# A sparse graph layer with gathered tiles: lists of 128-row tiles for any set of column groups, and products in one form

## The chip, the cores and the metric

One core of one Trainium2 chip. The metric is the device time of one execution in microseconds (us): the median of the runs of a kernel, taken beside runs of the other kernel on the same chip.

## The reference, cut to what matters

```
A_norm = relu((A + A.T) * 0.5)                 # A: 4096 x 4096, sparse, diagonal present
D = sum(A_norm, axis=1);  d = D ** -0.5        # 0 where D is 0
L_norm = I - d[:, None] * A_norm * d[None, :]
HW = einsum('bnf,fo->bno', x, W)               # x: 8 x 4096 x 256, W: 256 x 256
out = relu(einsum('nm,bmo->bno', L_norm, HW))
x = layernorm(x + out)                         # over the last 256 columns
```

The chance of an entry in A falls with the row's and the column's number, so the first rows are dense and most later ones thin. All numbers are f32.

## The kernel before

N = 4096 nodes are 32 blocks of 128. The 8 x 256 columns of HW are one row of G = 2048 numbers (8 KB) for each node, called g once it is scaled by d. An output block is the product of a 128-column strip of A (transposed, one row for each node m) with g; only nodes with an entry in the strip count.

**First part.** A is loaded in pieces of 512 x 512, symmetrised (transposes on PE, sums on DVE, L512 to L521) and written back to DRAM as `a_dram` (L523 and on). Beside it DVE and POOL keep `uses`: one flag for each row and each group of 32 columns. HW is formed (L596 to L645) and written as `g_dram`. Output block 0, the densest, is summed on the way as `lead` (L583). The lists of the first units are made here too, in pieces that are called by number (`due`, `run_due`, L676).

**Second part.** The other 31 blocks are handled in 16 units of two blocks, in the order SEQ. A unit has up to eight groups of 32 columns, four in each of its blocks b0 and b1. For each unit a list says which rows m are fetched and in which slot, so that rows that serve the same groups stand together. A tile is 128 slots. POOL fetches a tile by two indirect DMAs: `ga` (L1032: of each listed row of `a_dram`, 32, 128 or 256 columns, by `owner`) and `g` (L1047: the rows of g, 1 MB). Tiles lie in a ring of RING = 12 slots. The first blocks of g, which every unit needs, are kept on chip (`g_hub`, HUBS = 2 blocks in each unit); their strips of A, `gh`, come by small DMAs that POOL issues when the unit before has used the old ones (L1020).

A unit is a row of *steps*. A step is a list of products (t, half, b, j, w): tile t, rows of one half or of all 128, block b, w groups from group j. Each step runs them for four chunks of 512 columns (L1257 to L1270), so that a step fills the array of PE once for each chunk: one product of 128x128, two of 128x64, four of 128x32, two of 64x128, four of 64x64 or eight of 64x32. On the chip each f32 product shows as two instructions. `steps_of` (L878 to L937 and on) picks the forms: it looks at the next REACH = 8 tiles and takes the shape that fills the array best. Hub steps are woven between the others.

Before a unit starts, its lists are made on DVE and PE, several units ahead: `patterns` (which groups a row serves, as a number; then which of 15 KINDS of sets it belongs to), `count` (two products that rank the rows of each kind, L298), `place` (each row gets a slot in one of its kinds' half-tiles of L = 64 rows; rows that overflow go on to a pair or to a whole block by `offer`, L328), `count_rest` and `place_rest` (what is left over goes to tiles that serve all groups), `spread`, `collect` and `index` (slots are turned into row numbers by products with one-hot matrices, L450). The tables CAPS and FIRST give the half-tiles of each kind in each unit. Numbers that these need are written by small fills on POOL in the first part (`set_constants`, L215). At a unit's end, behind the last step with b0, PE gets the list products (`lists`, L1211).

After each step `gather_ahead` (L1057) asks for one more tile, or for two where more than SLACK = 5 slots are free; each request waits for that step's products. The results of a block are copied out of PSUM by ACT (`evict`, L788), and DVE does the residual and the layer norm.

If a list does not fit (`over`), a dense path computes everything again; for this input it does not run.

Of the kernel before, what the change touches and what calls it, by code (L numbers as in the profile page):

```python
# [9 lines left out]
F32 = mybir.dt.float32  # L10
# [11 lines left out]
KINDS = [15, 1, 4, 2, 8, 16, 64, 32, 128, 240, 51, 204, 60, 195, 0]  # L22
# [3 lines left out]
HUBS = [2] * 16  # L26

CAPS = [
# [16 lines left out]
]  # L45

FIRST = [
# [16 lines left out]
]  # L64
# [3 lines left out]
def kernel(  # L68
# [41 lines left out]
    RING = 12  # L110
    REACH = 8
    TAIL = 4
    SLACK = 5
    LONG = 28
    EPS = 1e-5
    NK = len(KINDS)
    L = 64
    mid = KINDS.index(16), KINDS.index(51)
    NL = NK - 1

# [4 lines left out]
    def upto_tile(u, ks):  # L125
        return max((FIRST[u][k] + CAPS[u][k] + 1) // 2 for k in ks)

    tiles = [upto_tile(u, range(NK)) for u in range(NU)]

    def owners(u, t):  # L130

        kinds_at = [k for k in range(NK) for s in (2 * t, 2 * t + 1) if FIRST[u][k] <= s < FIRST[u][k] + CAPS[u][k]]
        masks = [KINDS[k] or 255 for k in kinds_at]
        if all(m & (m - 1) == 0 for m in masks):
            return ALONE
        low, high = any(m & 15 for m in masks), blocks(u) == 2 and any(m >> QU for m in masks)
        return 2 if low and high else int(high)

    ALONE = 3
    owner = [[owners(u, t) for t in range(tiles[u])] for u in range(NU)]  # L140
    alone = [[t for t in range(tiles[u]) if owner[u][t] == ALONE] for u in range(NU)]
    tmax = max(tiles)
# [1257 lines left out]
```

## Time and profile before

| | |
|---|---|
| runs | 1496.15, 1495.63, 1490.57 us; median 1495.63 |
| profiled execution | 1496.15 us, span of the profile 1496.2 |
| first gathered product | 587 us |
| last product | 1484 us |
| PE busy, span | 1420.1 us (95%) |
| DMA | 540.52 MB, 361 GB/s on the mean |

The times in the prediction come from the one profiled execution. PE rows are matrix products, PEld rows the loads of their weights, which lie beside them. In rows of products by form, 128*32 is the part of the array that an instruction uses: rows by columns. Busy time is what the profile models for a product; products of different columns of the array lie beside each other, so a mean of 600 ns with four beside each other is not 600 ns of PE each.

### The profile page before, as it was taken

To read this page: it belongs to the slowest core of one execution; us is meant where nothing else is said; L and a number is where in the kernel's file an instruction comes from. 1 tells how busy PE (TensorE), PEld (TensorE's weight loads), DVE (VectorE), ACT (ScalarE), POOL (GpSimd) and SP (SyncE) were. 2 spreads that over 40 slices of the span, in tenths; PEclk is the share of its full clock that TensorE was granted. 3 is DMA by queue.
4 is the path that set the end of the run, shared out by engine and by line. 5 is a ranking of instruction groups with operands and counts; after the bars stand their busy time and mean duration, and the time that the engine had idled before them with its cause. 6 is when DMAs were issued, how large, how long until landed. Compare 5 with 4: busy or idle time off the path is not lost.

```text
span 1496.2 us, 20479 instructions
## 1 busy us (share of the span) xinstructions
PE 1420.1 (95%) x6768; PEld 757.9 (51%) x6768; DVE 1025.2 (69%) x3010; ACT 368.7 (25%) x462; POOL 745.6 (50%) x1547
## 2 busy tenths in 40 slices
PE   7998988979999999999999999999999999998996
PEld 6777877766777764333333334333333333333342
DVE  4767558889596752356569678789898079797454
ACT  4555545434544460010100100100110011001102
POOL 2444010010322336756577677577677646666762
PEclk9999999989999999999999999999999999999998
DMA  9999999999999999979899899999999979988995
GB/s 340 360 377 381 406 346 337 393 385 338 379 356 341 371 392 373 373 270 379 332 377 379 338 402 407 366 388 403 398 382 377 387 259 341 354 316 321 402 404 220
DMA packets 215265, 540.52 MB, mean 361 GB/s; under 512 B 17751, under 2 KB 107527, under 8 KB 180839
## 3 DMA queue, kind: packets, MB, share of 16 engines
q0 software_dynamic: 53808, 281.94, 48.5%
q1 hardware_dynamic: 93200, 126.62, 24.4%
q10 hardware_dynamic: 68144, 130.58, 23.0%
q8 instruction: 56, 0.92, 0.2%
q14 instruction: 57, 0.46, 0.1%
HBM read 425.72 MB, written 136.34 MB: 376 GB/s over the span
## 4 chain that ended last, share of the span: by engine, by line
PE 62%; DMA 14%; DVE 11%; issue 7%; POOL 3%; ACT 3%; ACTq 0%; another core or an unknown queue 0%; DVEq 0%; POOLq 0%; SPq 0%
PE py L1263 45%; PE pg L627 8%; DMA a_dram<-sym 6%; DVE sym L520 4%; DMA g<-g_dram,gi 3%; PE xtr L616 3%; PE lead L585 3%; PE tr L516 3%; DMA xin<-in_x_dram 2%; POOL ga L1032 2%; ACT sym L524 1%; DVE sums L527 1%; POOL g L1047 1%; DMA g_dram<-held 1%; PE lists L450 1%
## 5 line engine op out<-in xcount | busy, mean ns | idle before, releaser
L1263 PE MATMUL py<-g,ga 128*32 128x512 f32 (+4 forms) x2880 | 644.8, 606 | 12.3 <-DMA g<-g_dram,gi 7.2
L1263 PEld LDWEIGHTS py<-g,ga 128*32 128x32 f32 (+4 forms) x2880 | 226.0, 138 | 402.0 <-issue 374.4
L1032 POOL DMA_INDIRECT ga<-a_dram,ai x256 | 277.6, 1084 | 181.3 <-issue 62.2
L1047 POOL DMA_INDIRECT g<-g_dram,gi x256 | 284.5, 1111 | 92.9 <-issue 77.6
L788 ACT ACTIVATE y<-py,minus_r 128x512 f32<-128x512 f32 x120 | 80.2, 686 | 796.3 <-PE py L1263 545.9
L627 PE MATMUL pg<-w_sb,xt 128*128 128x256 f32 x1024 | 233.4, 387 | 6.5 <-ACT xt L617 5.7
L1263 PE MATMUL py<-g_hub,gh 128*128 128x512 f32 x496 | 226.6, 601 | 0.5 <-DVE low L465 0.3
L627 PEld LDWEIGHTS pg<-w_sb,xt 128*128 128x128 f32 x1024 | 196.9, 195 | 34.5 <-ACT xt L617 6.6
L520 DVE TENSOR_TENSOR sym<-tr,adj 128x512 f32<-128x512 f32 x256 | 162.3, 684 | 59.0 <-PE tr L516 54.1
L527 DVE TENSOR_REDUCE sums<-sym 128x64 f32<-128x2048 f32 x64 | 145.7, 2282 | 69.5 <-ACT sym L524 69.5
L528 POOL TENSOR_SCALAR uses<-sums 128x64 uint8<-128x64 f32 x64 | 26.7, 417 | 271.1 <-DVE sums L527 236.9
L516 PE MATMUL tr<-ident,adj 128*128 128x128 f32 x1024 | 137.1, 281 | 20.5 <-DVE sym L520 14.3
L1263 PEld LDWEIGHTS py<-g_hub,gh 128*128 128x128 f32 x496 | 90.5, 190 | 123.6 <-issue 116.8
L524 ACT ACTIVATE sym<-sym 128x2048 f32<-128x2048 f32 x64 | 122.7, 1917 | 122.8 <-DVE sym L520 118.6
L516 PEld LDWEIGHTS tr<-ident,adj 128*128 128x128 f32 x1024 | 115.8, 143 | 50.9 <-DVE sym L520 31.1
L242 DVE TENSOR_TENSOR_SCAN incl_r<-carry,lists 128x32 f32<-128x32 bf16 x13 | 2.9, 221 | 182.0 <-PE lists L397 176.0
L429 DVE TENSOR_TENSOR hot<-iota_q,at 128x1024 bf16<-128x1024 f32 x64 | 74.5, 1220 | 34.0 <-PE lead L585 32.1
L798 DVE TENSOR_TENSOR xr<-xr,y 128x2048 f32<-128x2048 f32 x31 | 70.8, 2284 | 38.8 <-ACT y L788 32.1
L616 PE MATMUL xtr<-ident,xin 128*128 128x128 f32 x512 | 74.5, 299 | 17.9 <-DVE sym L520 9.0
L831 DVE TENSOR_SCALAR xr<-xr,mv,root 128x256 f32<-128x256 f32 x248 | 85.1, 416 | 1.1
L807 DVE BATCH_NORM_STATS2 stats<-xr 128x6 f32<-128x256 f32 x248 | 84.0, 413 | 1.1
L585 PE MATMUL lead<-gt,strip 128*128 128x512 f32 x176 | 82.4, 593 | 0.0
(164 smaller groups left out, 1040.1 us busy)
## 6 DMA issues: line engine op xcount, KB each, us to landing
adj<-in_adj_dram SPq DMA_DIRECT2D x64, 1024.0 KB
a_dram<-sym ACTq DMA_DIRECT2D x64, 1024.0 KB
out_dram<-xr SPq DMA_DIRECT2D x31, 1024.0 KB
xr<-in_x_dram ACTq DMA_DIRECT2D x28, 1024.0 KB
xin<-in_x_dram SPq DMA_DIRECT2D x44, 512.0 KB
g_dram<-gt ACTq DMA_DIRECT2D x22, 1024.0 KB
xin<-in_x_dram POOLq DMA_DIRECT2D x20, 512.0 KB
g_dram<-held ACTq DMA_DIRECT2D x10, 1024.0 KB
```

The source lines that it names most:

```text
L516: ins = nc.tensor.transpose(pt[:, c * P : (c + 1) * P], tji[:, c, a * P : (a + 1) * P], ident)
L520: nc.vector.tensor_add(sym[:, a, :], pt, tij[:, a, :])
L524: nc.scalar.activation(sym, sym, AF.Relu, scale=0.5)
L527: nc.vector.tensor_reduce(sums, sym.rearrange("p a (c q) -> p a c q", q=E), AX.X, ALU.add)
L585: nc.tensor.matmul(lead[c], lhsT=strip, rhs=g[:, c * S : (c + 1) * S], start=not done, stop=len(done) == NB - 1, skip_group_check=True,)
L616: nc.tensor.transpose(pt[:, k, c, :], xin[b // H][:, b % H + k, c * P : (c + 1) * P], ident)
L627: ins = nc.tensor.matmul(pg[:, k * FO : (k + 1) * FO], lhsT=xt[:, b + k, c, :], rhs=w_sb[:, c, :], start=(c == 0), stop=(c == FC - 1),)
L807: nc.vector.bn_stats(stats[:, b, :], z[:, b, :])
L831: nc.vector.tensor_scalar(z[:, b, :], z[:, b, :], mv[:, b, 0:1], rstd[:, b : b + 1], ALU.subtract, ALU.mult,)
L1032: rows = nc.gpsimd.indirect_dma_start(out=at if both else at[:, : E if one else P], out_offset=None, in_=a_pairs if both else a_groups if ...
L1047: nc.gpsimd.indirect_dma_start(out=gt, out_offset=None, in_=g_dram, in_offset=bass.IndirectOffsetOnAxis(ap=gi[:, t : t + 1], axis=0), boun ...
L1263: return nc.tensor.matmul(py[2 * u + 1 + b][c][cols, :], lhsT=at[ps, off + cols.start : off + cols.stop], rhs=gt[ps, c * S : (c + 1) * S], ...
```

## The change

- A table UNITS gives for each unit: how many tiles hold rows of a single group (eight numbers), a list of tiles for sets of groups (mask, number, place), the number of tiles for the rest, the order (`turns`) in which tiles are used, how many of them a step may look at (`reach`), and by how much products of b1 are put behind those of b0 (`lag`). The mask may be any of the 255 sets. KINDS, CAPS, FIRST and the half-tiles are gone.
- `patterns` compares each row's set with every mask (`bitwise_and` against the mask's complement) and takes the fitting one with the highest weight (`match`). `place` gives out slots; rows that found no room get a second match among the masks with room left, with a count and a place of their own (`count_more`, `place_more`).
- Ranks come from two products that are summed in PSUM (`ranks`), which DVE reads there; `lower` includes the diagonal.
- The numbers that the lists need come as one inline table by DMA on ACT's queue; the POOL fills are gone.
- Each product has 128 rows and 32 columns, except those of hubs (128x128). `steps_of` first puts all hub steps of b0 and one of b1, then rounds of one product for each of the four column positions, then the other hub steps of b1.
- Hubs: three blocks in the first eight units by number, two in the others. The ring has 11 slots. `gather_ahead` asks for 1 + room // 3 tiles.
- In the first part, five units are begun instead of four (patterns and place of all five, the second place of four, the rest of three, two of them spread).

```diff
-HUBS = [2] * 16
+HUBS = [3, 3, 3, 3, 3, 3, 3, 3, 2, 2, 2, 2, 2, 2, 2, 2]
-    RING = 12
-    REACH = 8
+    RING = 11
-    SLACK = 5
+    SLACK = 3
+UNITS = [
...
+    (
+        [1, 1, 1, 1, 1, 1, 1, 1],
+        [(44, 1, 0), (145, 1, 1), (90, 1, 2), (246, 1, 3)],
+        1,
+        [0, 8, 1, 9, 2, 3, 10, 4, 5, 11, 6, 12, 7],
+        6,
+        6,
+    ),
...
-            for _ in range(room if behind is None else min(room, 1 + (room > SLACK))):
+            for _ in range(room if behind is None else min(room, 1 + room // SLACK)):
...
+    def steps_of(u):
+        _, _, _, turns, reach, lag = UNITS[u]
+        held = range(HUBS[u])
+        todo = {t: [(t, g // QU, g % QU, 1) for g in groups(masks[u][t])] for t in turns}
+        turn = {t: n for n, t in enumerate(turns)}
+        two = blocks(u) == 2
+        out = [full(-1 - h, 0) for h in held] + ([full(-1, 1)] if two else [])
+        while any(todo.values()):
+            near = [t for t in turns if todo[t]][:reach]
+            cells = sorted((op for t in near for op in todo[t]), key=lambda op: turn[op[0]] + lag * op[1])
+            step = []
+            for j in range(QU):
+                step += [op for op in cells if op[2] == j][:1]
+            for op in step:
+                todo[op[0]].remove(op)
+            out.append(step)
+        if two:
+            out += [full(-1 - h, 1) for h in held[1:]]
         return out
...
+    def match(n, u, pat, k, masks, by):
+        nc.vector.tensor_tensor(
+            beside, pat.unsqueeze(1).to_broadcast(full), masks.unsqueeze(2).to_broadcast(full), ALU.bitwise_and
+        )
+        nc.vector.scalar_tensor_tensor(
+            f, beside, 0.0, by.unsqueeze(2).to_broadcast(full), ALU.is_equal, ALU.mult
+        )
...
+        nc.vector.tensor_tensor(
+            kinds_in[n][:, :k, 1:], f, best.unsqueeze(1).to_broadcast(full), ALU.is_equal
+        )
...
-    def set_constants(u):
-        for k in range(NL):
-            nc.gpsimd.memset(limit[:, u, k : k + 1], float(CAPS[u][k] * L))
-            nc.gpsimd.memset(base[:, u, k : k + 1], float(FIRST[u][k] * L + 1))
...
+    tables = const.tile([P, ends[-1]], I32, name="tables")
+    nc.scalar.dma_start(tables, table.to_broadcast([P, ends[-1]]))
```

The first place is PE near the start of the second unit (unit 2; `py_2_0_1` is its block b0, chunk 1). Before, the end of a 128x32 step is followed by the second hub step and a step on a full tile:

```order
L1263 MATMUL py_2_0_3_6393<-g10_5767,ga10_5782 32x512
L1263 MATMUL py_2_0_3_6393<-g11_5771,ga11_5783 32x512
L1263 MATMUL py_2_0_3_6393<-g0_5727,ga0_5772 32x512
L1263 MATMUL py_2_0_3_6393<-g1_5731,ga1_5773 32x512
L1263 MATMUL py_2_0_0_6390<-g_hub1_5723,gh1_0_5786 128x512
L1263 MATMUL py_2_0_1_6391<-g_hub1_5723,gh1_0_5786 128x512
L1263 MATMUL py_2_0_2_6392<-g_hub1_5723,gh1_0_5786 128x512
L1263 MATMUL py_2_0_3_6393<-g_hub1_5723,gh1_0_5786 128x512
L1263 MATMUL py_2_0_0_6390<-g2_5735,ga2_5774 128x512
```

Now the last of four hub steps in a row is followed by a first round, and all that comes up to the unit's last hub steps is such rounds:

```order
L1272 MATMUL py_2_0_3_5672<-g_hub2_4947,gh2_0_5007 128x512
L1272 MATMUL py_2_1_0_5761<-g_hub0_4939,gh0_1_5004 128x512
L1272 MATMUL py_2_1_1_5762<-g_hub0_4939,gh0_1_5004 128x512
L1272 MATMUL py_2_1_2_5763<-g_hub0_4939,gh0_1_5004 128x512
L1272 MATMUL py_2_1_3_5764<-g_hub0_4939,gh0_1_5004 128x512
L1272 MATMUL py_2_0_0_5669<-g10_4991,ga10_5002 32x512
L1272 MATMUL py_2_0_0_5669<-g0_4951,ga0_4992 32x512
L1272 MATMUL py_2_0_0_5669<-g1_4955,ga1_4993 32x512
L1272 MATMUL py_2_0_0_5669<-g2_4959,ga2_4994 32x512
L1272 MATMUL py_2_0_1_5670<-g10_4991,ga10_5002 32x512
```

The hub steps moved ahead of the gathered ones, and each round opens with four tiles instead of one or two.

The second place is POOL's queue where the strips of A for the hubs of a coming unit are asked for (`gh`), between gathers for unit 2. Before, one strip stands between gathers:

```order
L1047 DMA g5_5747<-g_dram_75,gi_2_5176 128x2048
L1020 DMA gh0_0_5784<-a_dram_74 128x128
L1032 DMA ga6_5778<-a_dram_74,ai_2_5178 128x256
L1047 DMA g6_5751<-g_dram_75,gi_2_5176 128x2048
L1032 DMA ga7_5779<-a_dram_74,ai_2_5178 128x256
```

Now three stand nearly together, each waiting for the hub step that used the strip before it:

```order
L1028 DMA gh0_0_5003<-a_dram_74 128x128
L1041 DMA ga9_5001<-a_dram_74,ai_2_4582 128x256
L1056 DMA g9_4987<-g_dram_75,gi_2_4580 128x2048
L1028 DMA gh1_0_5005<-a_dram_74 128x128
L1028 DMA gh2_0_5007<-a_dram_74 128x128
L1028 DMA gh0_1_5004<-a_dram_74 128x128
L1041 DMA ga10_5002<-a_dram_74,ai_2_4582 128x256
```

Between the hub strips only a tile or none is asked for; the tiles come before and behind.

The third place is PE at the end of unit 1, the list products for later units (`lists2` for the rest, `lists0` and `lists1` for the kinds). Before:

```order
L396 MATMUL lists2_1_6170<-rest_4_5493,ones_87 128x32
L397 LDWEIGHTS lower_86
L397 MATMUL lists2_1_6170<-rest_4_5493,lower_86 128x32
L300 LDWEIGHTS ones_87
L300 MATMUL lists0_1_6168<-kind_5_5963,ones_87 128x448
L301 LDWEIGHTS lower_86
L301 MATMUL lists1_1_6169<-kind_5_5963,lower_86 128x448
```

Now:

```order
L500 MATMUL lists2_1_5454<-before_4_3972,ones_87 128x33
L501 LDWEIGHTS lower_86
L501 MATMUL lists2_1_5454<-rest_4_3969,lower_86 128x32
L409 LDWEIGHTS ones_87
L409 MATMUL lists1_1_5453<-ahead_of_1_115,ones_87 128x165
L412 LDWEIGHTS lower_86
L412 MATMUL lists1_1_5453<-kinds_in_1_113,lower_86 128x5x32
L409 LDWEIGHTS ones_87
L409 MATMUL lists0_1_5452<-ahead_of_0_114,ones_87 128x429
L412 LDWEIGHTS lower_86
L412 MATMUL lists0_1_5452<-kinds_in_0_112,lower_86 128x13x32
```

The pair for the second place, of 165 and 160 columns here, came in; the others stand as they did.

More of the change, by code (lines that the diff above doesn't have):

```diff
@@ L1 @@
 from contextlib import ExitStack, nullcontext
-from itertools import chain, groupby
+from itertools import groupby
+import numpy as np
 import concourse.bass as bass
@@ L109, with firsts, groups, owner @@
     HOLD = 10
-    RING = 12
-    REACH = 8
+    RING = 11
     TAIL = 4
-    SLACK = 5
+    SLACK = 3
     LONG = 28
     EPS = 1e-5
[L116 to L119, printed above, removed]
+    FIRST = NE + 7
+    NM = max(FIRST, *(len(kinds) for _, kinds, *_ in UNITS))
+    NC = G // S
+    M1 = NB + 1
     def blocks(u):
         return min(2, NB - 1 - 2 * u)
[L125 to L134, printed above, removed]
-            return ALONE
[L136 to L141, printed above, removed]
+    def firsts(u):
+        return min(len(UNITS[u][1]), FIRST - NE)
+    alone = [sum(UNITS[u][0]) for u in range(NU)]
+    masks = [
+        [1 << g for g in range(NE) for _ in range(UNITS[u][0][g])]
+        + [mask for mask, n, _ in sorted(UNITS[u][1], key=lambda kind: kind[2]) for _ in range(n)]
+        + [(1 << QU * blocks(u)) - 1] * UNITS[u][2]
+        for u in range(NU)
+    ]
+    tiles = [len(m) for m in masks]
+    ALONE = 3
+    def groups(mask):
+        return [g for g in range(NE) if mask >> g & 1]
+    def owner(u, t):
+        m = masks[u][t]
+        if m & (m - 1) == 0:
+            return ALONE
+        return 2 if m & 15 and m >> QU else int(m >> QU > 0)
     tmax = max(tiles)
@@ L177 @@
     nc.gpsimd.affine_select(
-        lower, ones, pattern=[[1, P]], compare_op=ALU.is_gt, fill=0.0, base=0, channel_multiplier=-1
+        lower, ones, pattern=[[1, P]], compare_op=ALU.is_ge, fill=0.0, base=0, channel_multiplier=-1
     )
@@ L204 @@
[L204 to L225 removed]
+    NT = NE + NM
@@ new lines @@
+    tiles_at = [sum(tiles[:u]) for u in range(NU)]
+    beyond = np.full((NU, NT), 1023, np.int32)
+    limits = np.zeros((NU, NT), np.float32)
+    starts = np.zeros((NU, NT), np.float32)
+    for u, (full, kinds, *_) in enumerate(UNITS):
+        at = 0
+        for g in range(NE):
+            beyond[u, g] = 1023 & ~(1 << g)
+            limits[u, g], starts[u, g] = full[g] * P, at
+            at += full[g] * P
+        for k, (mask, n, first) in enumerate(kinds):
+            beyond[u, NE + k] = 1023 & ~mask
+            limits[u, NE + k], starts[u, NE + k] = n * P, at + first * P
@@ new lines, in patterns, with ranks @@
+        nc.vector.tensor_scalar(none, pat, 0.0, 256.0, ALU.is_equal, ALU.mult)
+        code = t([P, NB], "code", I32, bufs=1)
+        nc.vector.tensor_add(code, none, pat)
+        k = NE + firsts(u)
+        match(0, u, code, k, beyond[:, u, :k], weight[:, NM - k :])
+        plan[u] = pat, code
+    def ranks(n, k, q):
+        nc.tensor.matmul(
+            q, lhsT=ones, rhs=ahead_of[n][:, :k], start=True, stop=False, skip_group_check=True
+        )
+        nc.tensor.matmul(
+            q[:, :, :NB],
+            lhsT=lower,
+            rhs=kinds_in[n][:, :k, 1:],
+            start=False,
+            stop=True,
+            skip_group_check=True,
+        )
@@ new lines, in count_rest, with place_rest @@
+    def count_rest(u, q):
+        _, rest, before = plan[u]
+        nc.tensor.matmul(q, lhsT=ones, rhs=before, start=True, stop=False, skip_group_check=True)
+        nc.tensor.matmul(
+            q[:, :NB], lhsT=lower, rhs=rest[:, 1:], start=False, stop=True, skip_group_check=True
+        )
+    def place_rest(u, q):
+        slot, rest, _ = plan[u]
+        room = UNITS[u][2] * P
+        first = tiles[u] - UNITS[u][2]
+        nc.vector.tensor_scalar(over[:, u : u + 1], q[:, NB : NB + 1], float(room), None, ALU.is_gt)
+        fits = ipool.tile([P, NB], F32, tag="fits1", name=f"fits1_{u}", bufs=1)
+        nc.vector.scalar_tensor_tensor(fits, q[:, :NB], float(room), rest[:, 1:], ALU.is_le, ALU.mult)
+        pos = ipool.tile([P, NB], F32, tag="pos1", name=f"pos1_{u}", bufs=1)
+        nc.vector.scalar_tensor_tensor(pos, q[:, :NB], float(first * P), fits, ALU.add, ALU.mult)
+        yield
@@ L1256, with product @@
         finish(0)
-        def product(u, op, c, ps, cols, start, stop):
-            t, _, b, _, _ = op
-            at, gt, apart, one = got[u, t] if t >= 0 else got[u, t, b]
-            off = -cols.start if one else b * apart
+        def product(u, op, c, first, last):
+            t, b, j, w = op
+            at, gt, who = got[u, t] if t >= 0 else got[u, t, b]
+            cols = slice(j * E, (j + w) * E)
+            off = -cols.start if who == ALONE else b * P if who == 2 else 0
             with queue("pe"):
```

667 lines of the change are left out of this document (313 added, 354 removed), and 32 rows, old and new, of tables (CAPS, FIRST).

## The prediction

> **What bounds the kernel now.** I read the page first: the shares of the engines, the 40 slices and the chain of work that ended last.
>
> ```profile
> span 1496.2 us, 20479 instructions
> PE 1420.1 (95%) x6768; PEld 757.9 (51%) x6768; DVE 1025.2 (69%) x3010; ACT 368.7 (25%) x462; POOL 745.6 (50%) x1547
> ...
> DMA  9999999999999999979899899999999979988995
> ...
> PE 62%; DMA 14%; DVE 11%; issue 7%; POOL 3%; ACT 3%; ACTq 0%; another core or an unknown queue 0%; DVEq 0%; POOLq 0%; SPq 0%
> ```
>
> PE is busy for 95% of the span and holds 62% of the chain, and nearly every slice of the DMA row shows a 9. Two resources lie close to their limit, so I split the span where the work changes. Stretches were asked for next: the span up to the first gathered product (587 us), from there to the last one (1484 us), and two pieces of the second part.
>
> ```profile
> core 0: us, PE busy (x) PEld busy (x) DVE busy (x) ACT busy (x) POOL busy (x), PEclk, DMA share, GB/s
> 0.00:587.00 587.00, 542.06 (x2894) 423.92 (x2895) 401.05 (x768) 280.61 (x329) 153.02 (x981) 0.97 0.99 368
> 587.00:1484.00 897.00, 878.05 (x3875) 334.00 (x3873) 619.01 (x2218) 83.27 (x126) 588.21 (x563) 0.99 0.95 361
> 857.00:947.00 90.00, 89.50 (x360) 34.13 (x360) 75.40 (x277) 5.50 (x8) 65.62 (x62) 1.00 1.03 403
> 1307.00:1397.00 90.00, 82.98 (x391) 32.16 (x385) 68.25 (x243) 8.24 (x12) 58.87 (x57) 0.96 0.90 327
> ```
>
> The first part is DMA's (share 0.99) with PE close behind (542 of 587). The second, 60% of the span, is PE's: 878 of 897 us busy. Here DMA carries 361 GB/s on the mean but 403 over the 90 us from 857, with PE busy all the same; it has some 10% in hand. Where PE falls behind, as from 1307, it stands beside a gather that is late: the waits of this part show what PE waits for, and the queue rows how much is fetched.
>
> ```profile
> PE py L1263 <- DMA g<-g_dram,gi: 7.2, 5, 2.8
> PEld py L1263 <- DMA g<-g_dram,gi: 19.8, 25, 1.7
> POOL ga L1032 <- PE py L1263: 51.3, 33, 10.5
> ...
> DMA packets 109230, 323.54 MB, mean 361 GB/s; under 512 B 12774, under 2 KB 75558, under 8 KB 79686
> ```
>
> PE waits 7.2 us for gathered tiles and its weight loads 19.8 us (part of that beside running products); POOL waits 51.3 us for PE to free a tile. So the ring is mostly full, and a step of products is what sets the pace: 234 steps in 897 us, 3.83 us each with all that lies between.
>
> What a step costs depends on its form. The products grouped by form, without the first 33 us (columns: instructions, then busy us and mean ns, then idle us before them):
>
> ```profile
> L1263 PE MATMUL py<-g,ga 128*128 128x512 f32 x632 | 286.8, 601 | 0.0
> L1263 PE MATMUL py<-g_hub,gh 128*128 128x512 f32 x472 | 215.6, 601 | 0.5 <-DVE low L465 0.3
> L1263 PE MATMUL py<-g,ga 128*64 128x512 f32 x670 | 152.4, 597 | 1.0 <-DMA g<-g_dram,gi 1.0
> L1263 PE MATMUL py<-g,ga 128*32 128x512 f32 x992 | 117.7, 595 | 3.1 <-DMA g<-g_dram,gi 2.7
> L1263 PE MATMUL py<-g,ga 64*32 64x512 f32 x384 | 44.9, 660 | 8.3 <-issue 4.0 <-DMA g<-g_dram,gi 3.6
> ```
>
> A step of full tiles is 8 of these instructions, one of 64-column products 16, one of 128x32 products 32. That makes 79, 59, 42 and 31 steps of 3.63, 3.65, 3.64 and 3.80 us. The last row is seven steps (four of 64 instructions, two of 48, one of 32) at 7.6 us each with their idle time: twice the price.
>
> Single steps, products alone:
>
> ```profile
> core 0: us, PE busy (x), PEclk, DMA share, GB/s
> 590.60:594.20 3.60, 3.60 (x33) 1.00 0.84 339
> 622.60:633.20 10.60, 10.60 (x34) 1.00 1.00 379
> 1466.30:1476.60 10.30, 10.30 (x25) 1.00 0.78 313
> 640.50:646.40 5.90, 5.90 (x65) 1.00 0.91 311
> 707.10:718.50 11.40, 8.75 (x65) 1.00 1.00 394
> 777.80:781.40 3.60, 3.60 (x49) 1.00 1.01 416
> 833.20:839.70 6.50, 5.95 (x51) 1.00 1.05 407
> 1290.60:1300.40 9.80, 8.30 (x65) 0.91 0.92 328
> 1342.30:1354.20 11.90, 8.35 (x66) 0.71 0.96 330
> 1413.50:1419.50 6.00, 5.47 (x27) 1.00 0.97 382
> ```
>
> The first is one 128x32 step: 3.60. The second holds three steps of forms that change (3.53 each), the third three full ones in a row (3.43 each). The next six are the 64x32 steps of 64 and 48 instructions: 5.9, 11.4, 3.6, 6.5, 9.8 and 11.9 us. The last is a 128x32 step that took 6.0 for no wait that the trace names.
>
> **The change part by part.** *Fewer steps.* Writing out the steps of both kernels gives 234 and 231: hub steps rise from 62 to 78 (a third block of g on chip in eight units), the others fall from 172 to 153. Three steps at 3.53: −10.6 us.
>
> *No 64-row products.* The seven 64x32 steps cost 5.9 + 11.4 + 3.6 + 6.5 + 9.8 + 11.9 = 49.1, and 3.6 for the small seventh (taken as one that kept pace): 52.7 us. As 128x32 steps at 3.60 they are 25.2. Of the 27.5 I take off 3.5: the step at 1342 shows a clock of 0.71 and stands where a gather was late, which the change does not cure. −24 us; the ends are −15 (only the stretches without a lower clock gain: 5.9 + 11.4 + 6.5 less three steps, 13, and a little of the rest) and −27.5.
>
> *All the rest as 128x32.* Of the 153 gathered steps 32 had that form; 121 take the place of full, 64-column and 64x128 ones. From below: in a run of equal steps the price may fall as in the full ones, 3.43 for 3.53, −12 us over 121. From above: the mean of the 128x32 steps, 3.80, against 3.63, +0.17 or +21 us; with its idle time, 3.90, +33. Most of that excess is the one step of 6.0 (2.4 us of it) and steps at a unit's end, where list products stand between; the undisturbed ones are 0.07 above the mixed row, each with a change of form on both sides, which a run of them has not. I take 0.
>
> [...]
>
> *Lists.* At a unit's end PE gets one more pair of list products. The pair it has, and their small sister:
>
> ```profile
> L301 PE MATMUL lists<-kind,lower 128*128 128x448 bf16 x12 | 4.2, 350 | 0.0
> L396 PE MATMUL lists<-rest,ones 128*128 128x32 bf16 x13 | 2.3, 181 | 0.0
> ```
>
> Two products of at most 165 columns lie between these rows, 0.18 to 0.35 each: about 0.4 us with their weight loads, in 12 units +5 us. On DVE the pattern lists lose a chain of some 40 small operations and gain a second match; DVE is busy 619 of 897 us, and I count nothing, as its lists are due a unit later. If that cover went, a late list would hold the gathers of a whole unit.
>
> *The ring.* A tile goes from twelve slots to eleven, POOL asks ahead by another rule, and the hub steps now stand together: three and one at a unit's start, two at its end. During these six steps (21 us) no tile is freed. POOL then has its 7 or so tiles to ask for in a burst, and what a tile costs is
>
> ```profile
> L1047 POOL DMA_INDIRECT g<-g_dram,gi x256 | 284.5, 1111 | 92.9 <-issue 77.6
> ```
>
> 1.1 us of POOL for g, as much for ga, and 1 MB. After the hub steps a 128x32 round opens four tiles at once. Eleven tiles are 31 us of transfers at 361 GB/s. A unit of some ten gathered steps (36 us) eats 15 tiles, 42 us of transfers; the six hub steps cover 21 us of these, less what x, the outputs and the hub pieces take. On the mean that closes, in a unit with many tiles barely. Bounds: 0 (all hidden) and +30 us (the 6 us by which 42 exceeds 36 lost in full in five units, those with the most tiles). I take +15, the middle. The traffic itself falls: written out for this input, 29,988 gathered rows of 8 KB become 29,164 (−6.8 MB), with one more hub block (+1 MB), 16 more hub pieces (+1 MB) and wider ga (+0.5 MB) that is −4.3 MB: 319.2 MB. Over the 882 us that my sum leaves this part it is 362 GB/s, the mean of now, so the traffic bounds nothing by itself, and its 12 us count only within the stall.
>
> *Before 587 us.* About 440 little fills of POOL fall away, and a table of 0.5 MB comes in on ACT's queue:
>
> ```profile
> L225 POOL MEMSET group_of<- 64x1 bf16 x304 | 29.1, 96 | 10.9
> L218 POOL MEMSET limit<- 128x1 f32 x224 | 13.6, 110 | 0.0
> ```
>
> POOL is busy 153 of 587 us there and no one waits for it: nothing. The table (128 rows of 928 words, 0.5 MB) is 1.3 us of DMA at 368 GB/s. A fifth unit's patterns and four second passes join DVE (401 of 587 busy). Between −5 and +8; I take 0. The first four products of a unit now need no gathered tile, which would hide a list that is up to 14 us later.
>
> Sum: −10.6 − 24 + 0 + 5 + 15 + 0 = −14.6. Against the profiled execution (1496.15, span 1496.2) that is 1481.6; the median of the runs, 1495.63, is 0.5 lower: 1481.
>
> **The rivals.** *The rounds run at 3.43.* [...] As a mechanism of this kernel: its forms change at most steps, and after the change two or three times a unit. With 0.10 saved in about 130 steps (−13) and a stall of 5 instead of 15: −14.6 − 13 − 10 = −38, 1458 us, for which DMA has to carry 319.2 MB in 859 us, 372 GB/s. For it speaks the row at 1466; against it that no two 128x32 steps stand next to each other before. 0.12.
>
> *The ring takes the gain back.* Eleven tiles and grouped hub steps: PE waits 0.5 to 1.4 us per unit longer than I took, +7 to +22 us over sixteen units, and −14.6 becomes −7 to +7: 1488 to 1503. For it speaks that 20 us of weight loads wait already and that the stretch from 1307 loses 7 us to late gathers with a slot more; against it the 51 us that POOL waits for PE. 0.17.
>
> *Dense rounds starve PE.* This is the side that is slower. The four long 64x32 steps and the 128x32 step at 1413 lose time without a wait; what they share is many small instructions (64 or 32 in products, as many weight loads). Seven to sixteen such rounds in a row need 18 instructions in each us, steadily. If a round costs 3.80, as the by-form row has it, the change is worth −14.6 + 26 (0.17 × 153) = +11, 1507; if one round in four stutters by 2.4, 38 × 2.4 − 14.6 = +77, 1572. It decides from 3.53 + 0.145: (14.6 + 7.5) / 153. For it speaks the row at 1413, against it the step of 48 at 777.8, which took 3.6 with half as many again. 0.26.
>
> **How the numbers follow.** A measurement of this kernel can tell about 0.5% (7.5 us) from no change. My forecast, 1465 to 1488, has 0.45; the rivals as given. Faster is the forecast and the first rival less a little that falls to either side: 0.57. The same: 0.17. Slower: 0.26. The range leaves out about 0.06 below (1452: half of the first rival) and 0.12 above (1530: the stutter in more than one round of six): 1452 to 1530. Both signs hold weight; the likeliest case by itself spans 1465 to 1488.
>
> **What would show it.** Products by form: one row of 128x32 with some 4,800 instructions; divided by 32 it should give 3.5 to 3.6 us a step; above 3.7 the third rival holds, at 3.45 the first. The waits: PE and its weight loads for gathered tiles at 20 to 45 us together if the ring is as I think, above 60 if the second rival holds. The first gathered product between 582 and 595 us; if later, a list was late, and my nothing for the first part was wrong. PE's idle time in the second part much above 35 us, or a chain in which POOL or DVE takes the place of PE, would make the whole account wrong.

## The result, and the profile after

The kernel after takes 1549.07 us (median of four runs, 1547.69 to 1554.74); the kernel before, beside it, 1495.89 (1490.57 to 1497.34). The ratio is 1.0362, 95% interval [1.0331, 1.0394]: 53 us slower, where 15 us faster was forecast. The profiled execution took 1550.08.

The page of after, its span, the shares of the engines and the chain of work that ended last:

```profile
span 1548.4 us, 23421 instructions
PE 1411.4 (91%) x8800; PEld 743.0 (48%) x8800; DVE 998.8 (65%) x2692; ACT 368.6 (24%) x462; POOL 672.0 (43%) x772
...
PE 19%; issue 18%; POOL 11%; DMA 8%; DVE 7%; another core or an unknown queue 5%; ACT 0%; POOLq 0%; ACTq 0%; DVEq 0%
```

PE is busy for 8.7 us less than before in a span that is 52.2 us longer, and its share of the chain fell from 62% to 19%. So PE did not get slower work; it stands. The stretches of after (columns as before), first the second part as a whole, then four and nine 128x32 rounds in a row:

```profile
core 0: us, PE busy (x) PEld busy (x) DVE busy (x) ACT busy (x) POOL busy (x), PEclk, DMA share, GB/s
0.00:591.70 591.70, 541.05 (x2904) 420.40 (x2905) 414.11 (x730) 279.25 (x329) 109.31 (x214) 0.97 0.99 364
591.70:1533.30 941.60, 870.14 (x5897) 322.55 (x5895) 579.46 (x1937) 84.34 (x125) 556.98 (x553) 0.98 0.92 341
...
617.78:631.52 13.74, 13.74 (x135) 7.15 (x130) 0.00 (x0) 0.00 (x0) 8.54 (x10) 1.00 1.01 399
...
1208.63:1239.55 30.92, 30.92 (x293) 11.90 (x288) 0.00 (x0) 0.00 (x0) 17.63 (x19) 1.00 0.98 387
```

The first part is 4.6 us longer, the products' part 45 (941.6 for 896.5), what follows the last product 2.5. Within the products' part PE stands idle for 71.5 us. Yet an undisturbed round is as cheap as the cheapest steps of before, the full ones in a row at 3.43: 13.74 / 4 and 30.92 / 9 are both 3.44 us. The products by form, without the first 33 us:

```profile
L1272 PE MATMUL py<-g,ga 128*32 128x512 f32 x4752 | 578.1, 606 | 28.1 <-DMA g<-g_dram,gi 21.3 <-issue 6.3
L1272 PE MATMUL py<-g_hub,gh 128*128 128x512 f32 x624 | 274.8, 596 | 4.8 <-DVE low L574 2.2 <-PE py L1272 1.7 <-ACT y L897 1.0
```

4,752 instructions are 148.5 rounds: 578.1 / 148.5 = 3.89 us, 4.08 with their idle time. The mean lies far above the undisturbed 3.44, so the loss is in some of the rounds. The waits of the second part (560 to 1540 us) say which:

```profile
POOL ga L1041 <- PE py L1272: 152.8, 59, 12.0
PEld L559 <- issue: 65.9, 56, 8.0
...
PE py L1272 <- DMA g<-g_dram,gi: 21.3, 11, 4.4
PE lists L559 <- DVE pos L514: 20.4, 5, 7.8
```

L559 stands for the one-hot products of `collect` (L450 before), which PE reaches right behind the list products at the end of a unit's b0. They wait for DVE (L514), up to 7.8 us at a time. All waits of PE ahead of L559 together come to 38.3 us; ahead of L450 they were 5.9, most of them here:

```profile
PE lists L450 <- DVE pos_r L247: 4.4, 10, 1.1
```

Such a place before, PE and then DVE (start, duration, operation, idle time before it and its releaser):

```profile
650.02 0.19 PE L396 MATMUL lists<-rest,ones 128*128 128x32 bf16 x1
...
650.99 0.43 PE L450 MATMUL lists<-val,hot 128*128 128x38 bf16 x11 [0.37 <-DVE pos_r L247]
```

```profile
650.27 0.22 DVE L242 TENSOR_TENSOR_SCAN incl_r<-carry,lists 128x32 f32<-128x32 bf16 x1 [38.41 <-PE lists L397]
```

And one of after, first PE, then DVE and POOL:

```profile
925.42 3.55 PE L1272 MATMUL py<-g,ga 128*32 128x512 f32 x28
928.90 0.19 PE L500 MATMUL lists<-before,ones 128*128 128x33 bf16 x1
...
929.29 0.37 PE L412 MATMUL lists<-kinds_in,lower 128*128 128x480 bf16 x1
937.42 0.46 PE L559 MATMUL lists<-val,hot 128*128 128x30 bf16 x11 [7.75 <-DVE pos L514]
```

```profile
936.81 0.16 DVE L510 TENSOR_SCALAR over<-lists 128x1 f32<-128x1 f32 x1 [26.11 <-remote]
...
937.18 0.18 DVE L514 SCALAR_TENSOR_TENSOR pos<-lists,fits 128x32 f32<-128x32 f32 x1
```

```profile
926.22 1.00 POOL L1056 DMA_INDIRECT g<-g_dram,gi  x1 [0.30 <-issue]
...
933.89 1.00 POOL L1056 DMA_INDIRECT g<-g_dram,gi  x1 [0.30 <-issue]
937.00 0.95 POOL L1041 DMA_INDIRECT ga<-a_dram,ai  x1 [2.10 <-remote]
```

DVE has been idle for 26 us and needs only the list products, which ran at 929. It starts at 936.81: the end of PE's work is *reported* (the semaphore that tells of it is raised) 7.9 us after L500 began, where before it took 0.25. In the trace's semaphore events the last product of 928.38 and all list products are reported together, at 936.74 to 936.92. Until 934.9 POOL issues gathers without a pause; its next one starts 0.2 us after DVE. PE restarts at half clock:

```profile
933.00:937.00 4.00, 0.00 (x0) 0.00 (x0) 0.19 (x3) 0.00 (x0) 1.59 (x2) 0.64 1.01 405
937.00:941.00 4.00, 3.58 (x19) 1.09 (x20) 3.93 (x14) 0.00 (x0) 1.95 (x2) 0.50 0.99 379
```

While the clock is 0.50 a product takes 0.85 us (starts at 937.80, 938.66 and 939.51) instead of 0.43 (941.10, 941.53 and 941.96).

Counted off by the program's order, the steps of the products' part show the bill, as the excess over 3.43 us a step (93.9 us in 234 steps before, 149.2 in 231 after):

| steps | before | after | difference |
|---|---|---|---|
| 13 with list products | 19.4 | 69.7 | +50 |
| other steps beside list or one-hot products | 14.6 | 27.0 | +12 |
| other gathered steps | 52.3 | 43.3 | −9 |
| other hub steps | 7.5 | 9.1 | +2 |
| three steps fewer | | | −10 |

The sum is +45. Before, DVE read the lists 0.25 us after the first list product's start in 12 of the 13 places (1.0 in the other). After: 2.8, 2.3, 1.5, 5.7, 7.9, 1.3, 0.7, 0.3, 4.9, 0.3, 0.3, 0.3 and 7.0 us. Ahead of each of the seven readings that come over 1.4 us late DVE had been idle for 9.5 us or more, so it is not DVE's own work that delays them.

### The profile page after: what moved, and what is told of

It reads as the page before. It is cut to its first block, busy times and chain, and to the rows that moved or that the text cites. A ratio compares the mean times of both kernels' runs of the same rounds, so it can differ in the third digit from the quotient of the medians.

```text
span 1548.4 us, 23421 instructions
## 1 busy us (share of the span) xinstructions
PE 1411.4 (91%) x8800; PEld 743.0 (48%) x8800; DVE 998.8 (65%) x2692; ACT 368.6 (24%) x462; POOL 672.0 (43%) x772
## 4 chain that ended last, share of the span: by engine, by line
PE 19%; issue 18%; POOL 11%; DMA 8%; DVE 7%; another core or an unknown queue 5%; ACT 0%; POOLq 0%; ACTq 0%; DVEq 0%
PE py L1272 13%; DMA g<-g_dram,gi 8%; POOL g L1056 5%; POOL ga L1041 5%; PE lead L692 3%; PE pg L734 2%; DVE hot L534 1%; DVE stats L916 1%; POOL gh L1028 1%; DVE xr L940 1%; DMA a_dram<-sym 1%; DVE xr L907 1%; PE tr L623 0%; PE xtr L723 0%
## 5 line engine op out<-in xcount | busy, mean ns | idle before, releaser
L1272 PE MATMUL py<-g,ga 128*32 128x512 f32 x4752 | 578.1, 606 | 28.1 <-DMA g<-g_dram,gi 21.3
L1272 PEld LDWEIGHTS py<-g,ga 128*32 128x32 f32 x4752 | 188.5, 112 | 394.4 <-issue 388.2
L1041 POOL DMA_INDIRECT ga<-a_dram,ai x243 | 252.5, 1039 | 257.8 <-PE py L1272 152.8
L1056 POOL DMA_INDIRECT g<-g_dram,gi x243 | 268.8, 1106 | 80.5 <-issue 73.4
L1272 PE MATMUL py<-g_hub,gh 128*128 128x512 f32 x624 | 274.8, 596 | 4.8 <-DVE low L574 2.2
L1272 PEld LDWEIGHTS py<-g_hub,gh 128*128 128x128 f32 x624 | 116.3, 190 | 145.6 <-issue 131.1
L724 ACT COPY xt<-xtr 128x512 f32<-128x512 f32 x128 | 67.7, 593 | 70.2 <-PE xtr L723 69.4
```

Of the source, the lines that this page charges most:

```text
L1041: rows = nc.gpsimd.indirect_dma_start(out=at[:, :width], out_offset=None, in_={2: a_pairs, ALONE: a_groups}.get(who, a_rows), in_offset=ba ...
L1056: nc.gpsimd.indirect_dma_start(out=gt, out_offset=None, in_=g_dram, in_offset=bass.IndirectOffsetOnAxis(ap=gi[:, t : t + 1], axis=0), boun ...
L1272: return nc.tensor.matmul(py[2 * u + 1 + b][c][cols, :], lhsT=at[:, off + cols.start : off + cols.stop], rhs=gt[:, c * S : (c + 1) * S], s ...
```

## The experiments

Theory: many small products and POOL's gathers together make PE's ends be reported late, so the lists, and then PE, stand. Rivals: the rounds themselves are slow, or it is the ring and its late tiles. All but four kernels (e9, e10, e17, e18) ran once, beside one or more runs of the kernel before, whose runs in all this work lie between 1478.6 and 1509.5; a single difference below some 15 us says little, and what the trace shows has to carry it. "Read" is the time from the first list product to DVE's reading, in the 13 places: how many over 1.4 us, and the longest. "List steps" are the 13 of the table above, "rounds" the other rounds of four tiles.

| run | us | before beside | read: over 1.4, longest | list steps, us | rounds, mean us | PE waits for g, us |
|---|---|---|---|---|---|---|
| before | 1495.9 | | 0, 1.0 | 64 | 3.75 | 7.2 |
| after | 1549.1 | 1495.9 | 7, 7.9 | 114 | 3.82 | 21.3 |
| e1 before, dense | 1527.2 | 1488.9 | 0, 1.2 | 73 | 3.86 | 3.3 |
| e2 after, wide | 1487.6 | 1488.9 | 0, 1.0 | 65 | 3.78 | 32.9 |
| e3 after, old asking | 1552.2 | 1488.9 | 5, 2.4 | 79 | 4.15 | 52.3 |
| e4 after, one-hot later | 1530.4 | 1488.9 | 6, 7.8 | | 3.85 | 27.0 |
| e5 after, no g | 1443.8 | 1489.5 | 0, 0.8 | 65 | 3.50 | 0 |
| e6 after, small g | 1535.5 | 1489.5 | 7, 8.4 | 116 | 3.65 | 4.5 |
| e7 after, half | 1509.2 | 1489.5 | 4, 9.0 | 88 | 3.72 | 20.6 |
| e11 after, g by SP | 1523.4 | 1490.2 | 0, 0.8 | 73 | 3.93 | 46.9 |
| e13 after, pause | 1551.5 | 1478.6 | 0, 0.3 | 68 | 4.31 | 61.1 |
| e14 after, long pause | 1577.3 | 1478.6 | 0, 0.3 | 68 | 4.45 | 71.6 |

**Width of the products.** In e1 the kernel before has its gathered products of 128 rows cut to 128x32:

```diff
+            cut = [
+                (t, i, b, e, 1) if t >= 0 and i is None else (t, i, b, j, w)
+                for t, i, b, j, w in step
+                for e in (range(j, j + w) if t >= 0 and i is None else (j,))
+            ]
...
-                for op in step:
+                for op in cut:
```

> The kernel before, with every gathered product over 128 rows cut into products of 32 columns; steps, tiles, gathers, ring and lists stay as they were. Theory D (runs of small products are what costs: PE reports their ends late, and those who wait for a report lose the time) expects most of the loss of the change here: 1525 to 1560 us, with the wait of DVE's list work for PE at a unit's end grown from 0.3 us to several. Rival G (POOL's bursts of up to four tiles) and rival R (eleven slots, hub steps together) expect no more than the 64-wide and full steps' own difference: 1490 to 1505 us.

```profile
L1263 PE MATMUL py<-g,ga 128*32 128x512 f32 x5056 | 604.8, 596 | 12.4 <-issue 10.0 <-DMA g<-g_dram,gi 0.2
```

38 us slower with the old lists, ring and order: 5,056 instructions are 158 rounds at 3.83, 3.91 with their idle time. The time is in the theory's range, but its mechanism is not there: the lists start on time. Of the 129 steps of 32 instructions that stand clear of list and one-hot products half take 3.55 us or less; the 25 that take over 4 us hold 48 of the 56 us above 3.43. In most of them single products start 0.5 to 1.4 us behind the one before instead of 0.4, without a wait that the trace names. So in e1 dense rounds cost time beside POOL's gathers with no list read later than 1.2 us.

e2 goes the other way: each round of after is one 128x128 product for each chunk, the four tiles in turn (so three quarters of the sums are left out).

```diff
-                for op in step:
-                    ins = product(u, op, c, opens[op], last[op])
+                if step[0][3] == QU:
+                    ins = product(u, step[0], c, opens[step[0]], last[step[0]])
+                else:
+                    t, b, _, _ = step[c % len(step)]
+                    ins = product(u, (t, b, 0, QU), c, False, False)
```

> The changed kernel, with each round of up to four 128x32 products replaced by one 128x128 product for each chunk (on the round's tiles in turn; the other groups' sums are left out). Lists, gathers, ring, hub steps and asking stay. Theory D expects 1549 to fall by 40 to 60 us, to 1490 to 1510, and the 7 us gaps ahead of the list products to go. Rivals G and R expect the gaps and the waits for tiles to stay: 1535 to 1550 us.

```profile
PE py L1274 <- DMA g<-g_dram,gi: 32.9, 16, 4.4
```

The lists are on time and the kernel stands where the one before does, with gathers, lists and hub order of after. The total is a single run, so whether a small gain is left without density it can't say; PE waits 32.9 us for late tiles.

e7 lies between: the same with two 128x64 products for each chunk (half of the sums left out).

> The changed kernel with each round of four 128x32 products replaced by two of 128x64 for each chunk (half of the groups' sums are left out): half the instructions. If the loss grows with the number of instructions, 1487 (one product) and 1549 (four) put this near 1505 to 1515 us; if there is a point from which it starts, above 9 instructions in each us, it stays at 1485 to 1495 us, without late reports.

1509, where a loss that grows with the number of instructions was put: four late places, two of them longer than any in after (9.0 us), the others within 0.4 us. So reports were up to 9.0 us late with products of 64 columns too.

**The gathers.** e3 puts the old rule of asking back:

```diff
-            for _ in range(room if behind is None else min(room, 1 + room // SLACK)):
+            for _ in range(room if behind is None else min(room, 1 + (room > 5))):
```

> The changed kernel, with the rule of before for asking ahead (one tile for each step, two where more than five slots are free). Rival G expects the gaps at the list products to go, 1500 to 1520 us. Theory D expects them to stay: 1545 to 1560 us, a little slower if tiles come later.

The reports are late by 2 us instead of 8, and PE waits 52.3 us for tiles instead of 21.3. The total stays. In e5, no g is gathered after the first eleven tiles (products run on old tiles); in e6 the instruction stays and fetches 512 bytes a row instead of 8 KB (the products use mostly old data).

> The changed kernel without the gathers of g after the first eleven tiles (products read what lies in the ring; 232 MB and as many POOL instructions are left out). Theory D1 (small products lose time by themselves, whatever else runs) expects the slow rounds and the late reports to stay: 128x32 steps without list products at a mean of 3.6 to 3.8 us, 1500 to 1530 us. Theory D2 (small products lose time only beside gathers) expects the rounds at 3.43 to 3.5 and reports within 0.3 us: 1455 to 1480 us.

> The changed kernel with the gathers of g cut to 512 bytes of each row after the first eleven tiles: POOL issues as many gathers with as many rows, but the bytes fall to a sixteenth. If D2 holds by what POOL does (its instructions, or the descriptors that it writes), slow rounds and late reports stay as in the change, 1510 to 1545 us; if by the traffic, they go as without the gathers, 1455 to 1485 us.

The products of e5 by form, and two waits of e6:

```profile
L1272 PE MATMUL py<-g,ga 128*32 128x512 f32 x4752 | 539.1, 593 | 2.5 <-issue 1.6 <-DMA ga<-a_dram,ai 0.8
```

```profile
PEld L559 <- issue: 67.8, 53, 9.1
...
PE py L1272 <- DMA g<-g_dram,gi: 4.5, 4, 1.6
```

Without g's gathers the same 4,752 instructions take 539.1 us (3.63 a round), and all lists start on time (0.8 us at the longest): rounds of 32-column products are not slow as such. With a sixteenth of g's bytes the late reports are all there (seven over 1.4 us, the longest 8.4). So in these runs it is POOL's gathers of g and not the bytes on the DMA engines; what of a gather does it, they do not separate. In e11 the same bytes come by plain DMAs on SP's queue, in fixed blocks instead of listed rows (other rows of g are multiplied):

```diff
+            if n >= RING:
+                with queue("sp"):
+                    ins = nc.sync.dma_start(gt, g_dram[t % NB * P : (t % NB + 1) * P, :])
...
-                nc.gpsimd.indirect_dma_start(
+                n < RING and nc.gpsimd.indirect_dma_start(
```

> The changed kernel, with g brought by plain DMAs on SP's queue after the first eleven tiles (128 rows that lie together in place of the listed ones, so the sums are others): the bytes stay, POOL's second gather of each tile goes. If POOL's gathers are what small products suffer from, and not the traffic, the reports come within 1 us and rounds cost 3.45 to 3.55: 1455 to 1490 us, the upper end if tiles come late. If the traffic counts after all, 1520 to 1550 us.

```profile
PE py L1282 <- DMA g<-g_dram: 46.9, 19, 4.7
```

The reports are on time (0.8 us at the longest). The kernel takes 1523.4 us all the same, above the 1490 expected: PE waits 46.9 us for tiles, which now come on SP's queue.

**A pause at the unit's end.** e13 keeps all gathers but asks for none in the last two steps with b0 and in the step of the list products, where the next three steps have their tiles:

```diff
-            gather_ahead(ins)
+            held_back = end0 - 1 <= q <= end0 + 1 and blocks(u) == 2
+            soon = {(v, op[0]) for v, st in steps[q + 1 : q + 4] for op in st if op[0] >= 0}
+            if not held_back or not all(at in got for at in soon):
+                gather_ahead(ins)
```

> The kernel after with no gathers asked for in the last two steps with b0 of a unit and the step of the list products (as long as the tiles of the next three steps have been asked for). Theory (POOL's indirect gathers, beside many 32-column products and the list products behind them, make PE's ends be reported late, so that DVE and then PE stand at a unit's end): the late starts of the lists on DVE, 2 to 7 us in six units, become at most 1 us in most of them, and of the 49 us of these steps 20 to 35 go; later gathers cost 0 to 15 us; 1515 to 1535 beside 1489 of the kernel before. Rival (the lateness comes from what PE has queued, whatever POOL does there): the late starts stay at 2 to 7 us, 1545 to 1560.

The place that was shown for after, here at 919 us, PE and then DVE; and a wait:

```profile
919.83 0.19 PE L500 MATMUL lists<-before,ones 128*128 128x33 bf16 x1
...
920.69 0.43 PE L559 MATMUL lists<-val,hot 128*128 128x30 bf16 x11
921.05 3.20 PE L1272 MATMUL py<-g,ga 128*32 128x512 f32 x14
```

```profile
920.09 0.16 DVE L510 TENSOR_SCALAR over<-lists 128x1 f32<-128x1 f32 x1 [19.71 <-PE lists L501]
```

```profile
PE py L1272 <- DMA g<-g_dram,gi: 61.1, 36, 4.2
```

DVE reads 0.26 us after L500's start, in this and the other twelve places, and PE goes on at 920.69, 0.1 us after the last list product. The list steps lose 46 of their 114 us, about all that can go (before they took 64). But the kernel is not faster: the other rounds rise from 432 to 487 us: tiles that were not asked for come late, and PE's waits for them go from 21.3 to 61.1 us. The mechanism was as expected, the time a miss. In four of the 13 places a gather that had been asked for earlier still runs while DVE reads, so what e13 takes away is the requests of these three steps, not every gather beside the lists. Holding the gathers for five steps (e14), and that with the one-hot products later (e15), adds only late tiles:

> As the run before, with the gathers held for five steps with b0 instead of two. Theory: if the gathers under way at the last product are what matters, the longer pause clears the late starts that the shorter one leaves, and costs more late tiles: 1510 to 1540. Rival: late starts as in the kernel after, and more late tiles: 1550 to 1575.

> The long pause, with the one-hot products for the lists begun one step later as in the run that did this alone (1530). Theory: both act on the same stops, so less than the sum of both: 1500 to 1525. Rival: the pause does nothing, 1530 to 1550.

1577.3 and 1567.0 us, above all that was expected, all lists on time in both, PE waiting 71.6 and 76.7 us for tiles. In e14 POOL gathers up to the list products all the same in several places (there from 922.44 to 932.4, behind 6 us without one; list at 929.33, read after 0.25 us); so in this place a gather beside them did not by itself delay the report.

**The one-hot products later.** e4 lets the first step behind the list products go ahead of the one-hot products, so that PE has work while DVE reads:

```diff
-                threads.append((collect(v, pl), -(-NB // room)))
+                after(2, threads.append, (collect(v, pl), -(-NB // max(1, room - 1))))
```

> The changed kernel, with the one-hot products of a unit's end started one step later, so that PE has a round of products to run while DVE waits for the report of the list products. Theory D expects the reports to be as late as before (DVE's list work starts 2 to 8 us after the list products in the same units) but PE to stand less: 1549 to 1505 to 1530 us. If it is the lists' own work on DVE that is late (rival L), the same gain comes, but with DVE busy in the gap.

> The kernel after with the same edit, again with an interval, beside the same runs of the kernel before. In the single run it stood 19 us below the kernel after: 1.020 to 1.030 of the kernel before if that holds; 1.033 to 1.040 if it was the chance of one run.

> The changed kernel with the asking rule of before and the one-hot products one step later. In the run with the rule alone the reports came up to 1.9 us late instead of 7, at 1552 us; in the run with the later products alone PE no longer stood for them, 1530 us. If the two losses are separate, both together give 1515 to 1525 us; if what the rule loses is tiles that come late, 1530 to 1545 us.

1530.4 in one run; with an interval (e18) 1539.56, ratio 1.0297 [1.0246, 1.0349] for after's 1.0362 [1.0331, 1.0394]: some 10 us of the 53, at intervals that still touch. The reports stay late (up to 7.9 us); PE does one step meanwhile. With the old rule of asking as well (e8) 1540.6: late reports of 2 us and 49.1 us of waiting for tiles. The same edit on the kernel before is the control:

> The kernel before with the one-hot products begun one step later, the control for that edit: before, the lists on DVE start on time, so both theories expect nothing to gain: 1485 to 1500 beside 1490 of the kernel before. If it gains 5 us or more, that edit takes more than the late reports with it.

> The kernel before with the one-hot products begun one step later, again, now with an interval. If the 12 us of the single run were this edit's (the one-hot products no longer stand between the list products and the next step, 0.5 to 0.7 us less for PE at each of 13 units' ends, 6 to 9 us): ratio 0.991 to 0.997. If they were the chance of one run: 0.998 to 1.003.

1466.1 beside 1478.6 in a single run, but 1499.77 beside 1494.73 with an interval, ratio 1.0024 [0.9996, 1.0053]: nothing, and a warning about single runs. The trace of e17 holds something else, though. Three of its 13 lists are read late, by 1.6, 3.1 and 1.6 us, after DVE had been idle for over 6 us. The longest, where the list products begin at 1059.68:

```profile
1062.75 0.22 DVE L242 TENSOR_TENSOR_SCAN incl_r<-carry,lists 128x32 f32<-128x32 bf16 x1 [6.16 <-remote]
```

Two of these places, the longest among them, stand behind steps of 128x128 and 128x64 products alone, beside gathers back to back. So here a report was 3.1 us late without the new lists and without 32-column products just before it; in after late ones come more often (seven) and are longer (up to 7.9).

**Two misses.** e9 cuts the four dense 64x32 steps of the kernel before in two steps of four products each; e10 adds the later one-hot products.

```diff
+            if len(pieces_) == 8:
+                rounds += [[p for p in pieces_ if p[2] == b] for b in range(2)]
```

> The kernel before, with its four steps of eight 64x32 products cut into two steps of four each, one for each block: as many instructions, at half the density, four steps more. These four cost 39 us in the profile of before. If density beside POOL's gathers is what makes them slow, eight steps at 3.5 to 3.6 come to 28 to 29 us: 8 to 13 us faster, ratio 0.991 to 0.995. If the 64-row form is slow by itself, eight steps of 64 instructions cost as much or more: ratio 1.000 to 1.010.

> As the last, and the one-hot products of a unit's end one step later, so that PE need not stand for DVE. PE's stop there is 1.3 us in thirteen units, of which list products are some 0.5: 5 to 9 us more, ratio 0.986 to 0.992. If the later products crowd into the steps that are left, no gain beside the last.

1506.2 and 1503.22 us, ratios 1.0109 [1.0072, 1.0146] and 1.0080 [1.0058, 1.0103]: longer by 1.1% and 0.8%, where a gain was expected. The trace of e9 shows that the steps themselves did what the first alternative said: the eight halves take 3.57 us each but for one of 4.28, 29.3 us where the four dense steps took 39.1. The time went elsewhere. Four rounds of 128x32 take 13.3, 7.8, 17.2 and 9.4 us (at 732, 1299, 1350 and 1419 us; e10 is slow at the same four), so that 35 rounds have a mean of 4.05 us instead of 26 at 3.75. In three of them PE waits for tiles that come late, for 6.8, 1.5 and 2.3 us, and two run at a mean clock of 0.74 and 0.70; what else lengthens them has no wait in the trace but "issue". The two longest:

```profile
740.20 5.46 PE L1267 MATMUL py<-g,ga 128*32 128x512 f32 x26 [6.83 <-DMA g<-g_dram,gi]
```

```profile
1357.64 1.88 PE L1267 MATMUL py<-g,ga 128*32 128x512 f32 x2 [3.88 <-issue]
1360.55 5.90 PE L1267 MATMUL py<-g,ga 128*32 128x512 f32 x26 [1.03 <-DMA g<-g_dram,gi]
```

e12 joins neighbouring products of one tile in a round to one of 64 or 128 columns, with the later one-hot products:

```diff
-            out.append(step)
+            out.append(joined(step))
```

> The changed kernel with neighbouring products of a round that read the same tile joined to one of 64 or 128 columns (594 products become 514), and the one-hot products one step later. Theory D expects the 60 us that density costs to fall by about a seventh, beside the 19 us that the later products gave: 1518 to 1526 us; without an effect of joining it stays at 1530 us, and with changes of form that cost 0.1 us each it goes to 1535 us.

1646 us, the largest miss. Two of its steps, each with one product of 64 columns and two of 32 for each chunk, in the stretches:

```profile
1279.90:1287.80 7.90, 7.90 (x25) 1.30 (x24) 0.00 (x0) 0.00 (x0) 1.95 (x2) 1.00 1.01 414
1287.80:1295.70 7.90, 7.90 (x26) 1.34 (x24) 0.00 (x0) 0.00 (x0) 1.95 (x2) 1.00 0.54 192
```

24 instructions take 7.9 us at full clock with PE busy throughout, where 32 of one width take 3.44. The starts in the trace say why: two 32-column products start within 0.01 us of each other, the 64-column one 0.45 to 0.52 us behind them, so in these steps the two widths take turns. There are 42 such steps; the 32 of them without list or one-hot products take 7.67 us on the mean, 136 us above 3.43 each. Four lists are also read late, by up to 6.6 us.

## Why the prediction was wrong

*Fewer steps, −10.6:* −10.3. Right.

*No 64-row products, −24:* the six steps were 28.5 us above 3.43 each, and they are gone; that was right for these steps, and in e9 too the split steps gain 10 us. The gathered steps as a group fell only from 52.3 to 43.3 us of excess, which is about this term and the ring's +15 taken together.

*All the rest as 128x32, 0:* the form's price is 3.44, which is what the rival "the rounds run at 3.43" had said; a gathered round in its company is 3.82. Between the two lie pauses as e1 shows them alone, and the late tiles. That rival's 0.10 a step is 3.53 less 3.43, both rows of before; that a change of form is its cause no run shows by itself. (The 121 of this term count the seven steps that the 64-row term has already; and the third rival charges 0.17 for all 153 rounds, though 32 had this form before, so its lower figure should have been +6 instead of +11. Neither changes the outcome.)

*Lists, +5:* **this is the step that failed**: "Two products of at most 165 columns lie between these rows [...] in 12 units +5 us", and of DVE, "I count nothing, as its lists are due a unit later". The products cost what I said: with the reports on time, in e13, the 13 steps take 68 us, before 64. But PE waits at this place for DVE's reading within the same unit (the one-hot products stand right behind), and DVE waits for PE's report. Reports had been on time in the rows that I read (0.25 us, once 1.0); in after they come up to 7.9 us late. Measured: +50 us in these steps and +12 beside them, for +5; that is more than the whole 53 us. That it is the lateness is shown by e13 (no late report, −46 us in these steps). It is where the time stood in after, though, not what punctual reports would give back: e13 as a whole is no faster, as its tiles come late instead. In these runs delays of after's size, 7.9 us, came only with POOL's gathers of g (e5 and e11, without them: 0.8 at the longest), with a sixteenth of their bytes as well (e6: 8.4), and only with products of 64 or 32 columns (e7, with 64: 9.0; e2, with 128: 1.0; e17 has one of 3.1 behind wider ones). These two are not all: e1 has both, with the old asking, ring and order, and reads its lists within 1.2 us. The way of asking is a part of the rest, by e3 (2 us late instead of 8).

*The ring, +15:* about right in after. PE waits 21.3 us for g where it had 7.2, 14 us more. With its weight loads (0.6 us, 19.8 before) it is 21.9, inside the 20 to 45 us that the prediction named as its sign. Where after's reports are made punctual and all of g still comes, PE waits 32.9 (e2) to 76.7 us (e15); that the stops at the lists had given the tiles time to come is likely, not shown. The second rival, "the ring takes the gain back", would fit e2's total (1487.6 beside 1488.9, one run each), but e2's waits, 45.2 us with the weight loads, stay below its sign of 60.

*Before 587 us, 0:* +4.6, within its bounds.

The third rival, dense rounds, had the side right, and its own test ("above 3.7 the third rival holds": 3.89) came out for it, but not its mechanism alone: in e5 the same rounds take 3.63. PE's idle time in the second part, 71.5 us for at most 35, was the other sign that the account was wrong.

Three things stay open. One is how POOL's gathers come to delay PE's reports. In five of the seven places of after that were read later than 1.4 us POOL stands still when the report comes, 1.4 to 1.9 us after its last gather, as if reports came through when POOL pauses; in the other two a gather is running, and e14's place at 929 us and four of e13 are on time beside running gathers, so no such rule holds. The trace has nothing on what lies between a product's end and its report. Another is what ends the pauses inside dense rounds for which the trace names no wait (e1, e9). The third is how much of the 53 us punctual reports alone would give back: each way to make them punctual with 32-column products and listed rows made tiles late instead, and a kernel that beats both was not found.

## What to carry to other kernels

In this kernel DVE's wait for PE's end cost what the *report* of that end took, and this was 0.25 to 7.9 us for the list products in the 13 places of after (0.3 at the longest in e13), depending on what else ran. So price a place where engine A waits for B, which waits for A, by its worst company, and put other work of A between the two (here that gave some 10 us of the 53, at intervals that touch). And when an undisturbed step is cheap and the mean is not, list the steps by what stands beside them before blaming the form.

## What the runs showed of the hardware that was not expected

- PE's ends, products and list products together, were reported up to 7.9 us late in after, beside 32-column products and POOL's indirect gathers (9.0 in e7 with 64-column ones). With 128-column products (e2: 1.0), without g's gathers on POOL (e5 and e11: 0.8) or with a pause in asking for them (e13: 0.3) none was over 1.0 us; e17, with the forms of before, has one of 3.1.
- An undisturbed round of 32-column products, 32 instructions, took 3.44 us (13.74 / 4 in after); one with a 64-column product and two of 32 columns for each chunk, 24 instructions, took 7.67 on the mean of 32 such steps of e12, the 64-column product starting 0.45 to 0.52 us behind the other two.
- A stop of PE of 7.75 us was followed by 3.6 us at a granted clock of 0.50 (937.4 to 941.0 us of after).
